# A graph layer on one Trainium2 core: edges sorted by POOL, a plan of old pairs moved by eight steps, a seed and an end on ScalarE

## The chip, the core and the metric

The kernel runs on one core of a Trainium2 chip. The core has five engines with instruction streams of their own: TensorE (PE), VectorE (DVE), ScalarE (ACT), GpSimd (POOL) and SyncE (SP), which here only issues DMAs. They meet at semaphores. SBUF is the core's working memory, PSUM holds the results of matmuls. The metric is the device time of one execution in microseconds, lower is better. Times are the median of several executions; beside them stands one execution that was recorded by the profiler, from which every duration below comes.

## What is computed

A graph with 6250 nodes and 100000 edges, 128 features each. For an edge with source `src` and destination `dst` a message is made of both nodes' features and the edge's own, normalised, passed through a relu and summed at the source node; the node's features are added and the row normalised again.

```python
x = _layernorm(x + _L0_gnn_ref(x, stack([src, dst]), edge_attr_128, W, b, gamma, beta))

def _L0_gnn_ref(x, edge_index, edge_attr, W, b, gamma, beta):
    row, col = (edge_index[0], edge_index[1])
    h = concatenate([x[row], x[col], edge_attr], axis=-1) @ W + b
    mu, var = mean(h), mean(square(h - mu))
    h = (h - mu) * rsqrt(var + 1e-5) * gamma + beta
    return segment_sum(relu(h), row, num_segments=6250)
```

The edges come sorted by destination, not by source.

## The kernel before

**Edges.** The 100000 edges are 782 tiles of 128, four to a slot, 196 slots `q` (0 to 195; the last has two tiles). In slot `q`, `edges(s, q)` (L610) makes the products of four tiles on PE, four fp32 matmuls at L619 for the edge's own features and four bf16 matmuls at L623 for the destination's; `evict` (L627) copies them to SBUF on ACT (L633); `scatters` (L639) sends each tile's 128 rows by an indirect DMA of POOL (L650) to their places in a DRAM table sorted by source. There are six tables, one for each split of the edges (`SPLITS`, L40): the last one, number 5, takes the tiles 704 to 781, slots 176 to 195.

**Ties.** Most scatters are tied to PE. At the end of slot `q`, `scatters(..., True)` issues the four tiles of slot `q - 1`, and ties them to the matmuls that PE was given since the last call (the list `done`, in which fp32 products weigh 4): the first tile to the matmul at a quarter of that work, the last to the last matmul of the slot. This holds up to slot 194; in slot 195 all that is left is issued untied. POOL's own queue is ordered by the scheduler, those of PE, DVE, ACT and SP are written out by hand. In both built programs the last four tied tiles stand in POOL's queue mixed with the six untied ones.

**Old pairs.** When a table is complete, its rows are read back by pairs of node blocks. There are 50 node blocks, so 25 pairs for a table. For the tables 0 to 4 (the old pairs) an item is one pair, or two (a twin); the last 17 items, 100 to 116, are table 4's: eight twins (100 to 107) and nine single pairs (108 to 116). `work(n)` (L1115) makes `n` steps; a step executes, for each item, those parts of its pipeline whose offset in `FLOW` (L1100) falls on this step. A new item enters every four steps. A single pair has its one-hot at offset 0 (`ones`, L748, DVE), the transposes at 2 (`turn`, L760, PE), their copy and the seed of a PSUM bank at 3 (`turned`, `seed`, L764, L770, ACT), the products with the sources' features at 5 (`pick`, L787, PE), the squares at 7 (L796, L799, ACT), the scaling at 9 (L805, L811, DVE), the sums at the nodes at 10 (`sums`, L820, PE) and their addition at 13 (`add`, L826, DVE).

**The plan.** How many steps are made in each slot follows from due points `(slot, step)` between which the plan runs straight (`due`, L1134, `steps_due`, L1139). The last two are (190, 432) and (197, 4 * 117 + ENDS); with ENDS = 0 this is (197, 468). In a slot, first come the edges' products, then one step, then the eviction, then the other steps, then the tied scatters. So what a plan changes is where the edges' products stand between the steps of the old pairs on PE, ACT and DVE. After the last slot, `work(n_tail - n_steps)` (L1245) makes the remaining steps up to number 474.

**The tail.** Table 5's 25 pairs are 14 units (`Unit`, L835) of 1, 2 x 11, 1 and 1 pairs. SP reads the rows of the first units (`load`, L843) as soon as the last scatter has landed. A unit goes through `ones`, `turn`, `turned`, `pick` (with a `seed` of the PSUM bank: an fp32 matmul with the identity on PE at L876, or a copy by ACT at L874), `square`, `root`, `scale`, `sums`, `add` as above. As its node blocks are then complete, it goes on to `begin` (times gamma), `stats`, `var`, `norm` and `end`, which scales and shifts the rows (on POOL at L972 and L973, or on DVE at L976) and issues the store of the result from SP (L978). The first unit's steps lie between the last eleven steps of the old pairs: step 474, `units[0].ones()`, step 475, `turn`, step 476, `turned`, step 477, `pick`, and so on (L1244 to L1265). At the very end the last three units b, d and c (b has two pairs, c and d one) are normalised and stored in the order b, d, c (L1295): b on POOL, d and c on DVE. The unit before them, a, is ended on POOL in both versions.

Of the kernel before, what the change touches and what calls it, by code (L numbers as in the profile page):

```python
# [12 lines left out]
AF = mybir.ActivationFunctionType  # L13
# [57 lines left out]
def col_bc(t, n):  # L71

    return t.unsqueeze(2).to_broadcast([t.shape[0], t.shape[1], n])
# [7 lines left out]
def flat(t):  # L81
    return t.rearrange("p t d -> p (t d)")


def fast_path(ctx, tc, io, bad_d, found):
# [3 lines left out]
    nc = tc.nc  # L89
# [157 lines left out]
    bias = const.tile([P, D], F32, name="bias")  # L247
# [472 lines left out]
    def load_pairs(s, p, n):  # L720

        k = 2 * SPLITS[s][1]
        rows = late["blk"].tile([P, KMAX, ROW], F32, name="hl", bufs=4)
        for i in range(n):
            nc.sync.dma_start(flat(rows[:, i * k:(i + 1) * k, :]),
                              dram_ap(sorted_d[s], (p + i) * k * P * ROW,
                                      [[k * ROW, P], [1, k * ROW]]))
        loaded[s, p] = rows
# [106 lines left out]
    class Unit:  # L835
# [130 lines left out]
            nc.vector.scalar_tensor_tensor(self.shift[:, :m], self.total[:, :m], -1.0 / D,  # L966
                                           self.frstd[:, :m], op0=ALU.mult, op1=ALU.mult)

        def end(self, last=False):
            y, m = self.y, self.m  # L970
            if not last:
                nc.gpsimd.tensor_tensor(y, y, col_bc(self.frstd[:, :m], D), op=ALU.mult)  # L972
                nc.gpsimd.tensor_tensor(y, y, col_bc(self.shift[:, :m], D), op=ALU.add)  # L973
            else:
                for j in range(m):
                    nc.vector.tensor_scalar(y[:, j, :], y[:, j, :], self.frstd[:, j:j + 1],  # L976
                                            self.shift[:, j:j + 1], op0=ALU.mult, op1=ALU.add)
            nc.sync.dma_start(io["out"][:, self.b0 * D:(self.b0 + m) * D], flat(y))  # L978
# [107 lines left out]
    n_steps = 0  # L1086
# [28 lines left out]
    def work(n):  # L1115

        nonlocal n_steps
        for _ in range(n):
            for off, step in FLOW:
                i = n_steps - LEAD - off  # L1120
                if i % 4 or not 0 <= i // 4 < len(pairs):
                    continue
                if step is None:
                    load_pairs(*pairs[i // 4])
                    continue
                if off == 0:
                    at_work[i // 4] = Pairs(i // 4, *pairs[i // 4])
                step(at_work[i // 4])
            n_steps += 1

    LEAD, ENDQ, ENDS = 6, 1, 0
    LAG = 5

    due = [(first_tile[s] // PT + LAG, 4 * first_item[s - 1]) for s in range(1, n_split)]  # L1134
# [67 lines left out]
    units = [Unit(sum(sizes[:i]), n) for i, n in enumerate(sizes)]  # L1202
# [41 lines left out]
    n_tail = 4 * (len(pairs) - 1) + LEAD + 4  # L1244
# [8 lines left out]
    work(1)  # L1253
    units[0].turned()
    work(1)
    units[0].pick(0)
    units[1].ones()
    work(2)
    units[1].turn()
    units[0].square()  # L1260
    work(5)
    assert not steps_at and not others and all(cleared[s] == NB // 2 for s in cleared)
    units[2].ones()
    units[4].load()
# [7 lines left out]
    a, b, c, d = units[-4:]  # L1272
# [21 lines left out]
    c.var()  # L1294
    for u in (b, d, c):  # L1295
        u.norm()
        u.end(u is not b)
    order.close()


@with_exitstack
def gnn_resnorm_kernel(ctx, tc, io):
    nc = tc.nc
    keep = ctx.enter_context(tc.tile_pool(name="keep", bufs=1))
    bad_t = keep.tile([1, 1], I32, name="bad_t")
    with ExitStack() as inner:
        found = []
        fast_path(inner, tc, io, bad_t, found)
    with tc.If(found[0] > 0, preferred_fallthrough_block=True, label="general"):
        with ExitStack() as inner:  # L1310
            general_path(inner, tc, io)
# [233 lines left out]
```

## Time and profile before

| what | value |
|---|---|
| median of 3 runs | 1114.98 us (1113.57 to 1116.06) |
| profiled execution | 1118.29 us |
| its span, first to last instruction | 1116.5 us |
| mean granted TensorE clock | 0.904 |
| HBM traffic | 220 GB/s over the span |
| largest group on POOL | L650, 782 scatters |
| largest groups on PE | L619 240.5 us, L820 231.3 us, L787 189.1 us |
| largest groups on ACT | L796 224.4 us, L633 113.4 us |

A row of a timeline has the start and the duration in us, the engine, line and operation, what it writes and reads, the number of instructions merged into the row, and in brackets the idle time of the engine before it and what ended it. A row of a table by windows has, for each engine, busy time and count, then the granted PE clock as a share of full speed, the DMA engines' share and GB/s. A row of grouped lines has the count, then busy us and mean ns of one, then idle time before.

### The profile page before, as it was taken

What the parts mean: (1) busy time and instruction counts of PE and PEld (TensorE: products, weight loads), DVE (VectorE), ACT (ScalarE), POOL (GpSimd) and SP (SyncE); (2) the same over time, 40 slices, a digit from 0 to 9 for tenths busy, and PEclk for the clock granted to TensorE, in tenths of its full rate; (3) what the DMA queues carried; (4) which work ended last, traced back from release to release, by engine and by line L of the source; (5) the groups of instructions that cost most, each with busy time, mean ns of one, the idle gap of its engine ahead of it and who ended that gap; (6) DMA issues with size and microseconds to landing.
All of it is one profiled execution on the core that took longest, in us unless ns stands there. A gap on an engine that the chain in (4) does not pass through costs nothing. (4 is left out here: it accounts for less than half of the span.)

```text
span 1116.5 us, 27245 instructions
## 1 busy us (share of the span) xinstructions
PE 868.9 (78%) x8880; PEld 805.1 (72%) x8880; DVE 846.0 (76%) x2364; ACT 754.6 (68%) x2983; POOL 798.5 (72%) x832
## 2 busy tenths in 40 slices
PE   6758656454887688788868688888989899987994
PEld 3657546444887678788868688887978788976773
DVE  7874656634687587768777687988898988877997
ACT  4324422115776667567767678887988999987995
POOL 2677777777777777777777777777777777774264
PEclk7788897666999899878989899998999999999998
DMA  7799999546787666667877648876877767744331
GB/s 218 230 274 267 287 312 295 185 157 205 246 282 223 218 207 204 224 205 242 277 236 239 209 147 290 268 228 223 256 245 241 232 200 248 250 144 136 124 122 61
DMA packets 128050, 247.20 MB, mean 221 GB/s; under 512 B 47005, under 2 KB 61231, under 8 KB 127897
## 3 DMA queue, kind: packets, MB, share of 16 engines
q1 hardware_dynamic: 101924, 191.92, 56.0%
q0 software_dynamic: 25104, 53.05, 13.3%
q8 instruction: 71, 1.16, 0.5%
q14 instruction: 81, 0.66, 0.2%
q10 hardware_dynamic: 870, 0.40, 0.1%
HBM read 155.49 MB, written 89.80 MB: 220 GB/s over the span
## 5 line engine op out<-in xcount | busy, mean ns | idle before, releaser
L650 POOL DMA_INDIRECT sorted<-hs,place_i x782 | 758.1, 969 | 251.0 <-issue 94.2
L787 PE MATMUL sel<-xa,ohn 128*128 128x128 bf16 x2550 | 189.1, 226 | 107.1 <-ACT sel L770 105.9
L619 PE MATMUL hp<-w,eT 128*128 128x128 f32 x1564 | 240.5, 303 | 22.0 <-ACT hs L633 22.0
L619 PEld LDWEIGHTS hp<-w,eT 128*128 128x128 f32 x1564 | 218.7, 214 | 53.0 <-issue 27.2
L787 PEld LDWEIGHTS <-ohn 128*128 128x128 bf16 x2550 | 165.4, 101 | 118.3 <-issue 99.8
L811 DVE SCALAR_TENSOR_TENSOR msg<-sel,rstd,cut 128x128 f32<-128x128 f32 x850 | 240.5, 345 | 7.9
L820 PE MATMUL pa<-msg,ohe 128*128 128x130 f32 x1700 | 231.3, 288 | 15.3 <-DVE acc L826 8.6
L796 ACT ACTIVATE sq<-sel 128x128 f32<-128x128 f32 x850 | 224.4, 282 | 27.8 <-PE sel L787 27.6
L820 PEld LDWEIGHTS pa<-msg,ohe 128*128 128x128 f32 x1700 | 210.8, 199 | 20.2 <-DVE acc L826 10.2
L796 ACT ACTIVATION_READ_ACCUMULATOR sq<-sel 128x1 f32 x850 | 180.9, 213 | 0.0
L748 DVE TENSOR_TENSOR ohe<-hl,beside 128x1024 f32<-128x1024 f32 (+2 forms) x117 | 130.2, 1113 | 21.4 <-DMA hl<-sorted 10.5
L633 ACT COPY hs<-hp 128x512 f32<-128x512 f32 x196 | 113.4, 580 | 43.5 <-PE hp L623 36.5
L770 ACT COPY sel<-hl 128x512 f32<-128x512 f32 (+1 forms) x225 | 128.1, 569 | 15.9 <-DVE msg L811 15.6
L568 ACT COPY hs<-sloc 128x12 f32<-128x12 f32 x66 | 14.1, 213 | 161.3 <-DMA sorted<-hs,place_i 158.7
L607 DVE TENSOR_SCALAR ohd<-db,part_w 128x512 bf16<-128x512 bf16 x192 | 69.1, 361 | 61.4 <-DMA db<-drel_d 47.2
L764 ACT COPY ohn<-tr 128x1024 bf16<-128x1024 bf16 (+2 forms) x117 | 107.8, 921 | 5.3 <-PE tr L760 5.3
L805 DVE RECIPROCAL rstd<-std 128x4 f32<-128x4 f32 (+1 forms) x225 | 38.2, 170 | 80.8 <-ACT std L799 79.7
L826 DVE TENSOR_TENSOR acc<-acc,pa 128x260 f32<-128x260 f32 x125 | 52.3, 418 | 54.4 <-PE pa L820 54.3
L623 PE MATMUL hp<-win,ohd 126*128 126x128 bf16 x782 | 82.0, 231 | 1.1 <-DMA win<-xb_d 1.1
L799 ACT ACTIVATE std<-ss,eps 128x4 f32<-128x4 f32 (+1 forms) x225 | 66.9, 297 | 7.3
L760 PE MATMUL tr<-ident_h,ohe 128*128 128x128 bf16 x850 | 69.4, 225 | 2.4 <-issue 2.0
L623 PEld LDWEIGHTS <-ohd 126*128 126x128 bf16 x782 | 66.2, 105 | 5.1 <-issue 1.4
(199 smaller groups left out, 1033.9 us busy)
## 6 DMA issues: line engine op xcount, KB each, us to landing
eT<-in_eT SPq DMA_DIRECT2D x96, 512.0 KB
hl<-sorted SPq DMA_DIRECT2D x75, 528.0 KB
db<-drel_d SPq DMA_DIRECT2D x96, 256.0 KB
sorted<-empty SPq DMA_DIRECT2D x100, 198.0 KB
hl<-sorted SPq DMA_DIRECT2D x50, 264.0 KB
sorted<-hs,place_i POOLq DMA_INDIRECT x782
hl<-sorted SPq DMA_DIRECT2D x25, 396.0 KB
sorted<-empty SPq DMA_DIRECT2D x50, 132.0 KB
```

Source lines behind the costliest of these rows:

```text
L619: pe(nc.tensor.matmul(hp[:, j, :], eT[:, at], w[:, 2, :], start=j == 0, stop=False, skip_group_check=True), 4)
L623: pe(nc.tensor.matmul(hp[:, j, :], oh[:3 * WN, at], win[:3 * WN, :], start=False, stop=j == m - 1, skip_group_check=True))
L633: nc.scalar.copy(hs[:, :m, 0:D], hp[:, :m, :])
L650: i = nc.gpsimd.indirect_dma_start(out=sorted_d[s][:, :], out_offset=bass.IndirectOffsetOnAxis(ap=place_i[:parts, t:t + 1], axis=0), in_=h ...
L748: nc.vector.tensor_tensor(self.ohe[:, :k, :], self.hl[:, :k, D:D + 1].to_broadcast([P, k, P]), row_bc(iota_p, k), op=ALU.is_equal)
L760: pe(nc.tensor.transpose(tr[:, j, :], half[:, j0 + j, 1::2], ident_h))
L764: nc.scalar.copy(self.ohn[:, :self.k, :], self.tr[:, :self.k, :])
L770: nc.scalar.copy(self.sel[g][:, :m, :], self.hl[:, j0:j0 + m, 0:D])
L787: pe(nc.tensor.matmul(sel[:, j, :], self.ohn[:, j0 + j, :], xa[:, b, i * D:(i + 1) * D], start=False, stop=j == m - 1 and i == 2, skip_gro ...
L796: nc.scalar.activation(sq[:, j, :], self.sel[g][:, j, :], AF.Square, accum_out=ss[:, j:j + 1])
L811: nc.vector.scalar_tensor_tensor(self.msg[:, j0 + j, 0:D], self.sel[g][:, j, :], rstd[:, j:j + 1], cut, op0=ALU.mult, op1=ALU.max)
L820: pe(nc.tensor.matmul(self.pa[:, h, :], self.ohe[:, i * k + j, :], self.msg[:, i * k + j, :], start=(j == h), stop=(j == k - 2 + h)), 4)
```

## The change

Four edits. (1) `ENDS` goes from 0 to 8: the plan's last due point is step 476 in place of 468 at slot 197, so that the old pairs' steps of the slots 190 to 195 come earlier against the edges. (2) The first unit of the tail has its PSUM bank seeded by a copy on ACT, not by a matmul on PE. (3) `end` takes an engine: b is ended on DVE in place of POOL, d on ACT in place of DVE, c on DVE as before. (4) The five steps behind the first unit are written as what is left up to step `n_tail + 11`, which is five in both versions.

```diff
-        def end(self, last=False):
+        def end(self, last=None):
             y, m = self.y, self.m
-            if not last:
+            if last is nc.scalar:
+                for j in range(m):
+                    nc.scalar.activation(y[:, j, :], y[:, j, :], AF.Identity,
+                                         bias=self.shift[:, j:j + 1],
+                                         scale=self.frstd[:, j:j + 1])
+            elif last is None:
                 nc.gpsimd.tensor_tensor(y, y, col_bc(self.frstd[:, :m], D), op=ALU.mult)
                 nc.gpsimd.tensor_tensor(y, y, col_bc(self.shift[:, :m], D), op=ALU.add)
             else:
...
-    LEAD, ENDQ, ENDS = 6, 1, 0
+    LEAD, ENDQ, ENDS = 6, 1, 8
...
-    units[0].pick(0)
+    units[0].pick(0, nc.scalar)
...
-    work(5)
+    work(n_tail + 11 - n_steps)
...
     for u in (b, d, c):
         u.norm()
-        u.end(u is not b)
+        u.end(nc.scalar if u is d else nc.vector)
```

## The prediction

> **What bounds the kernel now.** I read the page, then POOL's timeline around the last scatters, then what waited for them.
>
> ```profile
> span 1116.5 us, 27245 instructions
> L650 POOL DMA_INDIRECT sorted<-hs,place_i x782 | 758.1, 969 | 251.0 <-issue 94.2
> ```
> ```profile
> 1010.08 0.97 POOL L650 DMA_INDIRECT sorted<-hs,place_i  x1 [2.28 <-PE pa L820]
> 1011.42 0.96 POOL L650 DMA_INDIRECT sorted<-hs,place_i  x1 [0.37 <-PE sel L787]
> 1012.96 0.97 POOL L650 DMA_INDIRECT sorted<-hs,place_i  x1 [0.57 <-ACT hs L633]
> ...
> 1023.13 0.97 POOL L650 DMA_INDIRECT sorted<-hs,place_i  x1 [0.30 <-issue]
> 1024.40 0.87 POOL L650 DMA_INDIRECT sorted<-hs,place_i  x1 [0.30 <-issue]
> ```
>
> The page gives POOL 758.1 us of scatters, 0.97 us each. At the end they start 1024.40 - 1023.13 = 1.27 us apart when nothing holds them, so 782 of them fill 993 us: POOL paces most of the kernel. The row at 1024.40 is the last (tile 781, the shorter one). Counting back ten, 1011.42 is tile 771, the last of slot 192. The two rows before 1012 waited for PE: these scatters are tied to products. From 1012.96 to the end nothing waits, nine gaps of 1.27 us. So **the last scatter's start is the release of tile 771 plus ten gaps** (12.98 us, one of them 0.27 too long).
>
> What waits for the last scatter is the tail:
>
> ```profile
> 1026.54 19.64 SPq L847 DMA_DIRECT2D hl<-sorted  x15
> ```
> ```profile
> 1029.23 0.69 DVE L854 TENSOR_TENSOR ohe<-hl,beside 128x512 f32<-128x512 f32 x1 [0.95 <-DMA hl<-sorted]
> ```
>
> SP issues the first unit's load 1026.54 - 1024.40 = 2.14 us after the last scatter's start, and DVE's one-hot of it follows 2.69 us later, after an idle 0.95 us that ended with the load. DVE was there at 1028.28. So the load, and behind it POOL, already sets when the tail begins, by 0.95 us; whatever delays the last scatter delays the tail by as much.
>
> **The change, part by part.** *The plan.* The straight line from (190, 432) to (197, 468) gives 437, 442, 447, 452, 457, 462 steps after the slots 190 to 195; to (197, 476) it gives 438, 444, 450, 457, 463, 469. So the products of slot 193 come 3 steps later, of slot 194 5, of slot 195 6. The built program shows this order on PE, ACT and DVE; SP's order is the same. No instruction is added. What moves is the ties. Tile 771 is tied to the last PE product of slot 193. Before, that is the pick of step 451; after, the sums of step 456, for slot 193 now goes on to 456.
>
> ```profile
> 1003.20 1.11 PE L619 MATMUL hp<-w,eT 128*128 128x128 f32 x8
> 1004.15 0.39 PE L623 MATMUL hp<-win,ohd 126*128 126x128 bf16 x4
> 1004.37 1.11 PE L820 MATMUL pa<-msg,ohe 128*128 128x130 f32 x8
> 1005.32 0.83 PE L787 MATMUL sel<-xa,ohn 128*128 128x128 bf16 x12
> 1007.63 1.16 PE L820 MATMUL pa<-msg,ohe 128*128 128x130 f32 x8 [1.48 <-DVE acc L826]
> ...
> 1010.31 0.83 PE L787 MATMUL sel<-xa,ohn 128*128 128x128 bf16 x12
> 1010.98 1.11 PE L619 MATMUL hp<-w,eT 128*128 128x128 f32 x8
> 1011.93 0.39 PE L623 MATMUL hp<-win,ohd 126*128 126x128 bf16 x4
> 1012.15 0.39 PE L760 MATMUL tr<-ident_h,ohe 128*128 128x128 bf16 x4
> ...
> 1016.07 1.36 PE L820 MATMUL pa<-msg,ohe 128*128 128x130 f32 x8 [1.04 <-DVE msg L811]
> 1017.26 0.61 PE L619 MATMUL hp<-w,eT 128*128 128x128 f32 x4
> ...
> 1017.83 0.83 PE L787 MATMUL sel<-xa,ohn 128*128 128x128 bf16 x12
> ```
>
> The pick of step 451 is the row at 1010.31, done at 1011.14; POOL's 1011.42 follows it by 0.28. Slot 194's products are the rows at 1010.98 and 1011.93, slot 195's begin at 1017.26. The sums of step 456 are the row at 1016.07, done at 1017.43. In the changed kernel slot 194's products no longer stand in front of them: that takes away 12.15 - 10.98 = 1.17 us of PE. But slot 193's products (1003.20 to 1004.54) now come after step 449, that is just ahead of the pick at 1010.31. Where they stood they cost nothing, since PE soon after idled 1.48 us for DVE's addition; where they go, no such wait follows, and they cost their 1.17 us there. So the two nearly cancel: the sums of step 456 end at about 1017.1 (I take 0.3 us off for the copy of an eviction, ACT's smaller part). Bounds: 1016.1 if slot 193's products stay hidden, 1017.4 if nothing is saved. Then tile 771 starts at 1017.1 + 0.3 = 1017.4, and the last scatter, ten gaps of 1.27 later, at 1030.1: **5.7 us later** (4.7 to 6.0). The other ties bind less: slot 194's last one, the sums of step 460, lies some 3 us behind 1017.4, and its tile is sixth behind it in the queue, 7.6 us later. Slot 195's eviction, which feeds the last two, lies well ahead too. DVE, at the first unit's one-hot near its old 1028.3, waits until 1029.23 + 5.7 = 1034.9. Steps 475 to 485 stand behind that one-hot on DVE, so nothing useful fills the hole, and the whole tail shifts.
>
> *The clock in the hole.*
>
> ```profile
> 1028.86 0.83 PE L787 MATMUL sel<-xa,ohn 128*128 128x128 bf16 x12
> ```
>
> This is PE's last product that needs nothing of the first unit, the pick of step 475, done at 1029.69. In the changed kernel PE then has nothing until the first unit's one-hot (1034.9 + 0.69) is made, from about 1030 to 1035.6.
>
> ```profile
> 349.04 0.85 PE L787 MATMUL sel<-xa,ohn 128*128 128x128 bf16 x12 [4.47 <-ACT sel L770]
> ```
> ```profile
> 411.54 1.44 PE L787 MATMUL sel<-xa,ohn 128*128 128x128 bf16 x12 [5.11 <-ACT sel L770]
> ```
> ```profile
> 411.00:412.00 1.00, 0.46 (x5) 0.46 (x5) 0.00 (x0) 1.00 (x6) 0.74 (x1) 0.58 0.20 68
> ...
> 414.00:415.00 1.00, 1.00 (x10) 0.94 (x10) 1.00 (x3) 1.00 (x8) 0.76 (x1) 0.71 0.78 276
> ```
>
> Such holes are in the trace: after 4.47 us of idling the twelve products of a pick took 0.85 us, after 5.11 us they took 1.44, at a granted clock that fell to half within the microsecond 411 and came back within 414. With a hole of 5 to 5.6 us I take the second row: half clock for the first 3 us of the tail. In these stand only the first unit's four transposes (the size of the row at 1012.15: 0.39, so 0.27 more by the ratio of the two picks) and sums that follow DVE; the first unit's pick comes some 3 us after the transposes (the row at 1032.93 below, 3.0 behind the end of its one-hot). I put 0.2 us. Bounds: 0, and 1.3 if it lasts 5 us (the pick 1.44 - 0.85 = 0.6 more, the transposes of two units, about 1 us, by the same ratio 0.7). The Trainium skill, in "TensorE: Matmul & The Clock Gate", section Part 1, states the rule behind it: the clock halves after an idle window of about 3.4 us, and the window runs free, so its phase decides. By that rule the hole that this change opens would be paid for twice in something over half the executions; the rows above agree that near 5 us either can come.
>
> *The seed on ACT.*
>
> ```profile
> 1032.08 0.30 ACT L799 ACTIVATE std<-ss,eps 128x4 f32<-128x4 f32 x1
> 1033.80 0.28 ACT L898 ACTIVATE sq<-sel 128x128 f32<-128x128 f32 x1 [1.43 <-PE sel L887]
> ```
> ```profile
> 1032.07 1.02 PE L876 MATMUL sel<-hl,ident 128*128 128x512 f32 x2
> 1032.93 0.83 PE L887 MATMUL sel<-xa,ohn 128*128 128x128 bf16 x12
> ```
> ```profile
> L874 ACT COPY sel<-hl 128x512 f32<-128x512 f32 x2 | 1.2, 592 | 0.0
> ```
>
> PE loses 1.02 us of seed. ACT reaches its copy after the root at 1032.08, so at 1032.38, and is done 0.59 later at 1032.97: the pick starts where it did. The copy lies in ACT's idle 1.43 us. I count 0 (between -0.1 and +0.1 around it; if that cover were gone, 0.59).
>
> *The end.*
>
> ```profile
> 1106.69 0.17 DVE L966 SCALAR_TENSOR_TENSOR shift<-total,frstd 128x4 f32<-128x4 f32 x1
> ...
> 1107.23 0.56 DVE L966 SCALAR_TENSOR_TENSOR shift<-total,frstd 128x2 f32<-128x2 f32 x1
> 1107.83 1.40 DVE L976 TENSOR_SCALAR y<-y,frstd,shift 128x128 f32<-128x128 f32 x2
> 1109.15 0.15 DVE L964 RECIPROCAL frstd<-fstd 128x2 f32<-128x2 f32 x1
> 1109.41 0.16 DVE L966 SCALAR_TENSOR_TENSOR shift<-total,frstd 128x2 f32<-128x2 f32 x1
> 1109.60 0.60 DVE L976 TENSOR_SCALAR y<-y,frstd,shift 128x128 f32<-128x128 f32 x2
> ```
> ```profile
> 1107.85 1.04 POOL L973 TENSOR_TENSOR y<-y,shift 128x512 f32<-128x512 f32 x1
> ```
> ```profile
> L955 ACT ACTIVATE sq<-y,total 128x128 f32<-128x128 f32 x50 | 19.5, 390 | 3.2 <-DVE y L945 3.2
> ```
>
> Two DVE instructions take 1.40 us while POOL runs its 1.04, and 0.60 without it; a shift takes 0.56 in place of 0.16. So POOL's end of b costs DVE 0.8 + 0.4 = 1.2 us. Taken off POOL, b adds four scalings to DVE: 0.60 for two, 0.26 apart, gives 1.12 for four, from 1106.86 to about 1107.98. Then d's reciprocal and shift (1109.15 to 1109.60: 0.45) to 1108.43, then c's and its two scalings (1.05) to 1109.48, against 1110.20: **0.7 us off** (bounds 0 and 1.2). ACT ends d beside it: two instructions like L955, 0.78 us, to about 1109.2, ahead of c. The stores follow in the same order on SP.
>
> **Sum:** +5.7 + 0.2 + 0 - 0.7 = +5.2 us. The profiled execution would go from 1118.29 to 1123.5. It was 3.3 us above the median; I put the same sum on the median: 1114.98 + 5.2 = **1120.2 us**.
>
> **Rivals.** (a) *The extra steps partly fill idle time*, so tile 771's tie is later by less: five steps are 1.25 single pairs. From the pick at 1010.31 to the one that begins right behind slot 195's products, at 1017.83, two pairs and two slots' products share 7.52 us; less 1.17 and 0.57 for the products this is 2.9 a pair, so 3.6 for five steps: the tie ends at 1011.14 + 3.6 = 1014.7, the last scatter comes 3.3 us later (one gap's 0.27 is gone): 1114.98 + 3.3 - 0.7 = 1117.6. Against it: slot 193's products lose their free place.
> (b) *Not slower.* All of the moved work falls into idle time ahead of tile 771.
>
> ```profile
> 1000.00:1010.00 10.00, 7.08 (x76) 6.50 (x74) 6.72 (x22) 6.11 (x26) 5.40 (x6) 1.00 0.32 102
> ```
>
> From 1000 to 1010 ACT is busy 6.11 us and DVE 6.72 of 10, so 3.3 to 3.9 us are idle, and five steps take 3.6 us by (a). Then 771 keeps 1011.42 and only the end counts: 1114.3. It decides if the sums of step 456 end before about 1011.9. Against it: the idle time comes from additions, sums and scalings that wait for one another in a written order, which more steps do not shorten.
> (c) *The half clock lasts 5 us* and costs 1.3 in place of 0.2: 1121.3.
> (d) That the plan does nothing is ruled out by the order of the built program; edit (4) does nothing.
>
> **How the numbers follow.** Forecast 0.57 (own range 1118.5 to 1121.0: the tie's bounds, the end's, and about 1 us of scatter between runs); (c) 0.14; (a) 0.14; (b) 0.15. Differences within 0.2% (2.2 us: 1112.8 to 1117.2) are about what a measurement of this kernel cannot tell from none. Slower: forecast, (c) and 0.08 of (a), 0.79. Same: 0.06 of (a) and 0.10 of (b), 0.16. Faster: 0.05, the part of (b) for gains that I have no price for. The range takes in (a) and (c) and leaves (b) out: 1115.8 to 1122.0.
>
> **What would show it.** Right: POOL's last scatter some 5 to 6 us later against the first unit's surroundings, its wait for L820 in front of the last ten longer; DVE's wait for the first load near 6 us in place of 0.95; no L973 in the last 5 us and L976 at 0.3 us each. Wrong: a wait for the load still under 1 us with the last scatter where it was (then b), or scatters that start at less than 1.27 us, or a tail that is shorter from the first one-hot on, which would say that the seed mattered.

## The result, and the profile after

| | before | after |
|---|---|---|
| median of six runs each | 1115.26 us (1113.57 to 1117.65) | 1122.78 us (1119.40 to 1124.45) |
| ratio | | 1.0059, 95% interval 1.0044 to 1.0075 |
| profiled execution, its span | 1118.29, 1116.5 us | 1123.85, 1122.0 us |

The changed kernel is slower by 4.9 to 8.4 us (the interval times 1115). The ratio is estimated from all runs and is not the quotient of the medians, which is 1.0067; the medians are 7.52 us apart. The forecast was 5.2 us more; the profiled pair differs by 5.56 us, its spans by 5.5. The median itself, 1122.78, lies 0.8 us above the upper end of the range. Runs of one kernel are 4 to 5 us apart, and each kernel has one trace on this chip. Part of what the traces lack against the medians can be seen in them. PE of both kernels, the kernel before first, at the last products that stand in the same order in both:

```profile
996.99 0.39 PE L760 MATMUL tr<-ident_h,ohe 128*128 128x128 bf16 x4
```
```profile
994.96 0.39 PE L760 MATMUL tr<-ident_h,ohe 128*128 128x128 bf16 x4
```

PE of the changed execution is 2.03 us ahead there. It was as far ahead at 964.30 (966.34 in the kernel before), where the plans are still the same, so this head start is not the change's. Counted from these transposes, the end of the span comes 127.04 us later in the changed kernel and 119.51 before: 7.53 us more.

The page of the changed kernel: its span, and the scatters (busy, mean ns, idle before them).

```profile
span 1122.0 us, 27246 instructions
L650 POOL DMA_INDIRECT sorted<-hs,place_i x782 | 758.1, 969 | 255.8 <-issue 109.0
```

The scatters are as busy as before (758.1 us) and POOL waits 255.8 - 251.0 = 4.8 us longer ahead of them. POOL's timeline shows where: the second row is tile 771, ten places ahead of the last.

```profile
1014.26 0.96 POOL L650 DMA_INDIRECT sorted<-hs,place_i  x1 [0.45 <-PE tr L760]
1016.94 0.96 POOL L650 DMA_INDIRECT sorted<-hs,place_i  x1 [1.72 <-PE pa L820]
1018.30 0.96 POOL L650 DMA_INDIRECT sorted<-hs,place_i  x1 [0.40 <-issue]
...
1028.48 0.97 POOL L650 DMA_INDIRECT sorted<-hs,place_i  x1 [0.30 <-issue]
1029.75 0.86 POOL L650 DMA_INDIRECT sorted<-hs,place_i  x1 [0.30 <-issue]
```

Tile 771 started at 1011.42 after a pick (L787); now it starts at 1016.94 after the sums (L820). From there to the last scatter nothing waits: 1029.75 - 1016.94 = 12.81 us, ten gaps. The sums on PE that release it, and the evictions on ACT that feed the tiles behind it (slots 194 and 195):

```profile
1015.30 1.36 PE L820 MATMUL pa<-msg,ohe 128*128 128x130 f32 x8 [1.04 <-DVE msg L811]
```
```profile
1017.81 0.59 ACT L633 COPY hs<-hp 128x512 f32<-128x512 f32 x1 [0.90 <-PE hp L623]
1021.17 0.36 ACT L633 COPY hs<-hp 128x256 f32<-128x256 f32 x1
```

The sums end at 1016.66, 0.28 ahead of the scatter. Slot 194's rows are ready at 1018.40, before the second scatter behind tile 771 starts, and slot 195's at 1021.53, 7 us before the scatter at 1028.48 takes the first of them. So the tie holds POOL here, not an eviction. What waits for the last scatter, on SP's queue and on DVE:

```profile
1031.89 20.67 SPq L847 DMA_DIRECT2D hl<-sorted  x15
```
```profile
1034.78 0.69 DVE L854 TENSOR_TENSOR ohe<-hl,beside 128x512 f32<-128x512 f32 x1 [6.71 <-DMA hl<-sorted]
```

DVE is at the first unit's one-hot at 1028.07 (before: 1028.28) and now waits 6.71 us for the load, where it waited 0.95. The loss is one wait at one place.

To add it up I divide the end of both executions at four points; all are starts of rows but the fourth:

| stretch | before | after | difference |
|---|---|---|---|
| up to the first unit's one-hot (L854) | 1029.23 | 1034.78 | +5.55 |
| from there to its squares (L898) | 4.57 | 5.42 | +0.85 |
| from there to b's reciprocal (L964) | 72.68 | 72.67 | -0.01 |
| from there to the end of DVE's last instruction | 3.72 | 2.77 | -0.95 |
| from there to the end of the span | 6.30 | 6.36 | +0.06 |

The sum is +5.5 us, the difference of the spans; the first stretch has the head start of 2.03 us in it. The second stretch is the clock's. PE, then ACT, at the tail's start in the changed kernel:

```profile
1028.64 0.83 PE L787 MATMUL sel<-xa,ohn 128*128 128x128 bf16 x12
1035.53 0.61 PE L864 MATMUL tr<-ident_h,ohe 128*128 128x128 bf16 x4 [6.06 <-DVE ohe L854]
1038.66 1.44 PE L887 MATMUL sel<-xa,ohn 128*128 128x128 bf16 x12
```
```profile
1037.83 0.30 ACT L799 ACTIVATE std<-ss,eps 128x4 f32<-128x4 f32 x1
1038.03 0.58 ACT L874 COPY sel<-hl 128x512 f32<-128x512 f32 x1
1040.20 0.28 ACT L898 ACTIVATE sq<-sel 128x128 f32<-128x128 f32 x1 [1.59 <-PE sel L887]
```
```profile
1033.00:1034.00 1.00, 0.00 (x0) 0.00 (x0) 0.00 (x0) 0.00 (x0) 0.00 (x0) 0.80 0.97 264
1034.00:1035.00 1.00, 0.00 (x0) 0.00 (x0) 0.22 (x1) 0.00 (x0) 0.00 (x0) 0.50 1.00 346
...
1039.00:1040.00 1.00, 1.00 (x12) 1.00 (x10) 0.96 (x5) 0.00 (x0) 0.00 (x0) 0.50 0.41 68
1040.00:1041.00 1.00, 1.00 (x13) 1.00 (x12) 0.23 (x1) 0.80 (x7) 0.00 (x0) 0.79 0.93 330
```

The windows (each row is one microsecond, with the granted clock third from the right) put the clock at half from about 1033.6 to 1040.4. In it the transposes take 0.61 in place of 0.40 and the pick 1.44 in place of 0.83. ACT's root (L799) follows the one-hot by 3.05 us, where it was 2.85: the 0.2 of the transposes. The pick adds 0.61. Together 0.81 of the 0.85.

The end, on DVE and ACT (b's reciprocal is at 1112.87):

```profile
1113.08 0.16 DVE L966 SCALAR_TENSOR_TENSOR shift<-total,frstd 128x4 f32<-128x4 f32 x1
1113.28 1.11 DVE L981 TENSOR_SCALAR y<-y,frstd,shift 128x128 f32<-128x128 f32 x4
1114.30 0.16 DVE L964 RECIPROCAL frstd<-fstd 128x2 f32<-128x2 f32 x1
1114.50 0.16 DVE L966 SCALAR_TENSOR_TENSOR shift<-total,frstd 128x2 f32<-128x2 f32 x1
1114.58 0.17 DVE L964 RECIPROCAL frstd<-fstd 128x2 f32<-128x2 f32 x1
...
1115.04 0.60 DVE L981 TENSOR_SCALAR y<-y,frstd,shift 128x128 f32<-128x128 f32 x2
```
```profile
1114.69 0.88 ACT L973 ACTIVATE y<-y,shift,frstd 128x128 f32<-128x128 f32 x2 [0.22 <-DVE shift L966]
```

Four scalings take 1.11 us where two took 1.40 beside POOL. DVE is done at 1115.64, 2.77 after b's reciprocal, and ACT's part (to 1115.57) lies beside it.

### The profile page after: what moved, and what is told of

Read it like the earlier page. It is cut to its first block, busy times and chain, and to the rows that moved or that the text cites. A ratio compares the mean times of both kernels' runs of the same rounds, so it can differ in the third digit from the quotient of the medians.

```text
span 1122.0 us, 27246 instructions
## 1 busy us (share of the span) xinstructions
PE 872.9 (78%) x8878; PEld 809.7 (72%) x8878; DVE 846.8 (75%) x2366; ACT 754.9 (67%) x2986; POOL 796.4 (71%) x830
## 3 DMA queue, kind: packets, MB, share of 16 engines
q8 instruction: 71, 1.16, 0.4%
## 5 line engine op out<-in xcount | busy, mean ns | idle before, releaser
L650 POOL DMA_INDIRECT sorted<-hs,place_i x782 | 758.1, 969 | 255.8 <-issue 109.0
L787 PE MATMUL sel<-xa,ohn 128*128 128x128 bf16 x2550 | 190.6, 227 | 100.6 <-ACT sel L770 99.3
L787 PEld LDWEIGHTS <-ohn 128*128 128x128 bf16 x2550 | 166.9, 102 | 111.9 <-issue 95.8
L820 PE MATMUL pa<-msg,ohe 128*128 128x130 f32 x1700 | 234.1, 291 | 15.9 <-DVE acc L826 9.5
L820 PEld LDWEIGHTS pa<-msg,ohe 128*128 128x128 f32 x1700 | 213.8, 202 | 20.5 <-DVE acc L826 11.5
L799 ACT ACTIVATE std<-ss,eps 128x4 f32<-128x4 f32 (+1 forms) x225 | 66.9, 297 | 7.3
```

Source lines behind the costliest of these rows:

```text
L650: i = nc.gpsimd.indirect_dma_start(out=sorted_d[s][:, :], out_offset=bass.IndirectOffsetOnAxis(ap=place_i[:parts, t:t + 1], axis=0), in_=h ...
L787: pe(nc.tensor.matmul(sel[:, j, :], self.ohn[:, j0 + j, :], xa[:, b, i * D:(i + 1) * D], start=False, stop=j == m - 1 and i == 2, skip_gro ...
L820: pe(nc.tensor.matmul(self.pa[:, h, :], self.ohe[:, i * k + j, :], self.msg[:, i * k + j, :], start=(j == h), stop=(j == k - 2 + h)), 4)
```

## The experiments

Theory T: the loss is the tie. Five more steps stand ahead of tile 771's product, the last scatter moves by that, and DVE waits for the load. Rival E: slot 194's and 195's products and evictions were moved too, and they would hold POOL as long without the tie. Rival C: the half clock in PE's hole costs more than the 0.2 that I gave it. Rival S: the seed or the end costs, not the plan.

All experiments ran on other chips than the pair above. On these the kernel before takes 1349 to 1363 us: the engines have further idle stretches of up to 17 us there that the profile puts down to "remote", and the HBM rate is 180 GB/s in place of 220. Why is not known. Each ratio below is to the kernel before on the same chip, so it stands; but most kernels there have no wait for the first load, and this limits what they could tell. The changed kernel itself was not run there.

**The plan alone** (e1_plan; e1b_plan is the same kernel on another chip).

```diff
-    LEAD, ENDQ, ENDS = 6, 1, 0
+    LEAD, ENDQ, ENDS = 6, 1, 8
...
-    work(5)
+    work(n_tail + 11 - n_steps)
```

> Edits (1) and (4) alone: the plan's last due point at step 476, seed and ends as before. Theory (the ties move with the plan, so POOL's last scatters and behind them the first load come later): DVE waits 6 to 7 us for the first unit's load (0.95 before, 6.71 with the whole change), the clock is at half when the tail begins, the stretch from the first one-hot to b's last reciprocal is about 0.8 us longer than before's 77.25, and the end is before's 3.73 from b's reciprocal to the last DVE instruction; so the time is some 6 to 8 us above before, more than with the whole change by the 0.95 that the end gave. Rival (the loss comes from the seed on ACT or from the ends): a wait near 1 us and a time near before's.

> The plan alone (ENDS = 8) once more, to have it on the same chip as the kernels beside it. Theory: 6 to 8 us above before; DVE waits 6 to 7 us for the first load, the last scatter starts 4.8 to 5.1 us ahead of the first one-hot as in before and after, the stretch from that one-hot to b's last reciprocal is 77.9 to 78.3 us at a half clock in its first 3 to 6 us, and 3.7 us follow to the last DVE instruction. Rival: a wait near 1 us.

Measured: 1367.62 against 1363.2 us, 1.0055 (1.0027 to 1.0083); the second time 1352.15 against 1348.73, 1.0024 (1.0002 to 1.0045). POOL, then DVE, of e1_plan:

```profile
1254.04 0.97 POOL L650 DMA_INDIRECT sorted<-hs,place_i  x1 [2.32 <-PE pa L820]
...
1267.68 0.87 POOL L650 DMA_INDIRECT sorted<-hs,place_i  x1 [0.30 <-issue]
```
```profile
1274.35 1.13 DVE L811 SCALAR_TENSOR_TENSOR msg<-sel,rstd,cut 128x128 f32<-128x128 f32 x4
1275.39 0.68 DVE L854 TENSOR_TENSOR ohe<-hl,beside 128x512 f32<-128x512 f32 x1
```

The first half of T is as in the changed kernel: tile 771 (1254.04) waits for the sums L820. The second half isn't there: the one-hot's row has no bracket, it follows DVE's scaling at once, 7.71 us after the last scatter (9.72 in the second trace). DVE itself comes too late for the load to matter. So the plan alone is slower on two chips, and the wait for the load is not the reason there. From the one-hot to the first unit's squares (L898) it is 6.27 and 5.63 us in these traces, and 4.83 in e2_end and e6_untied, which have the old plan and the same seed; so 0.8 to 1.4 us may lie there. The cause stays open.

**The end alone** (e2_end), **the seed alone** (e3_seed), **both** (e4_seed_end).

```diff
-        u.end(u is not b)
+        u.end(nc.scalar if u is d else nc.vector)
```
```diff
-    units[0].pick(0)
+    units[0].pick(0, nc.scalar)
```

> Edit (3) alone: b ended on DVE, d on ACT, c on DVE; plan and seed as before. Theory: from b's reciprocal to the last DVE instruction 2.8 us in place of 3.73 (measured with the whole change: 2.78), nothing else moves, so about 0.9 us less time (0.08%), too small for the ratio but plain in the timeline. Rival: the stores of the last units set the end, and the distance from the last DVE instruction to the end of the span grows by what DVE saves (6.29 us before: 1116.5 less 1110.21).

> Edit (2) alone: the first unit's seed as a copy on ACT. Theory: the first unit's pick starts 3.7 us after its one-hot as before (1029.23 to 1032.93), so nothing is gained or lost, within 0.15 us, and the stretch from the first one-hot to b's last reciprocal stays at 77.25 within 0.3 us. Rival: that stretch gets longer by 0.6 us or more, which would put the 0.84 us that it grew with the whole change on the seed, not on the clock.

> Edits (2) and (3) without the plan (ENDS = 0). Theory: the sum of both, about 0.9 us faster than before (0.1%), DVE's wait for the first load about 1 us, the clock at full when the tail begins. Rival (seed or end carry part of the loss): slower than before by 2 us or more.

Measured, against 1363.2: e2_end 1363.59, 1.0001 (0.9976 to 1.0026); e3_seed 1362.71, a single time without an interval; e4_seed_end 1363.22, 1.0011 (0.9987 to 1.0035). Totals tell nothing at this size, but the stretches do. From b's reciprocal to DVE's end it is 2.77 or 2.78 us in all nine traces with the new end, and 3.71 to 3.73 in all five without it: the end is worth 0.95 us up to there. After that, up to the end of the span, it is 5.6 to 6.4 us with either, so no row shows the gain lost again. The seed is seen in PE's and ACT's rows, e2_end first:

```profile
1279.84 1.02 PE L876 MATMUL sel<-hl,ident 128*128 128x512 f32 x2
1280.69 0.83 PE L887 MATMUL sel<-xa,ohn 128*128 128x128 bf16 x12
```
```profile
1280.15 0.30 ACT L799 ACTIVATE std<-ss,eps 128x4 f32<-128x4 f32 x1
```

and then e3_seed:

```profile
1277.64 0.83 PE L887 MATMUL sel<-xa,ohn 128*128 128x128 bf16 x12 [0.36 <-ACT sel L874]
```
```profile
1276.81 0.30 ACT L799 ACTIVATE std<-ss,eps 128x4 f32<-128x4 f32 x1
1277.01 0.58 ACT L874 COPY sel<-hl 128x512 f32<-128x512 f32 x1
```

The root stands 3.41 us behind the one-hot in both. With the seed on PE the pick comes 1280.69 - 1280.15 = 0.54 after the root, with the copy 0.83 after it, and waits for the copy. So the seed on ACT costs 0.29 us there; e4_seed_end has the same 0.83. With the new plan it is the other way round: in both traces of the plan alone, seed on PE, the pick comes 1.25 us after the root (1279.54 to 1280.79 in e1_plan). Rival S falls as a cause of a loss of several us.

**Untied** (e5_plan_untied: the changed kernel; e5b_plan_untied the same on another chip; e6_untied: the kernel before). The scatters of the slots from 191 on are issued without a tie.

```diff
-    TIE = (12, 195)
+    TIE = (12, 191)
```

> The whole change, but the scatters from slot 191 on are issued right behind their slot's eviction and are not tied to PE products (TIE ends at 191). Theory (the ties carry the delay, not the evictions): POOL's last scatter is held only by the evictions of slots 194 and 195, so it comes 4 to 6 us earlier against DVE's arrival at the first one-hot than in the whole change; DVE's wait for the load falls from 6.7 to 1 to 3 us, the clock stays full, and the time is 4 to 6 us below the whole change. Rival (later evictions alone delay the scatters): the wait stays at 5 us or more and the time at the whole change's.

> The whole change with the scatters from slot 191 on untied, again, since on the chip of the first try the engines came later than the load in every kernel. Where the kernel before takes near 1115 us: theory (the ties carry the delay) a wait of DVE for the first load of 1 to 3 us in place of 6.7, a full clock at the tail's start, a stretch of 77.3 to 77.7 us from the first one-hot to b's reciprocal, and a time 4 to 6 us below the whole change, that is within 2 us of before. Rival (evictions): wait 5 us or more, time 5 us or more above before. Where before takes 1340 us or more: no wait in either, and nothing is told apart.

> The kernel before (ENDS = 0, seed and ends as they were) with the scatters from slot 191 on untied. Theory: POOL runs them 1.27 us apart from slot 191 on and wins the 3.2 us that it idled in front of the last ten; DVE then reaches the first one-hot before or with its load, so its wait of 0.95 us goes and about 1 us (0.1%) is gained, no more, since DVE's own work ahead sets the start. Rival (the ties spare PE or the DMA engines something): the work ahead of the tail gets longer and the time rises by 2 us or more.

Measured: e5_plan_untied 1355.92 against 1348.73, 1.0045 (1.0013 to 1.0077); e5b_plan_untied 1367.85 against 1363.03, 1.0033 (1.0008 to 1.0059); e6_untied 1354.24 against 1348.73, 1.0032 (1.0003 to 1.0061). POOL's waits in e6_untied:

```profile
1227.17 0.96 POOL L650 DMA_INDIRECT sorted<-hs,place_i  x1 [3.54 <-ACT hs L633]
...
1244.98 0.96 POOL L650 DMA_INDIRECT sorted<-hs,place_i  x1 [7.59 <-ACT hs L633]
...
1251.40 0.97 POOL L650 DMA_INDIRECT sorted<-hs,place_i  x1 [1.64 <-ACT hs L633]
```

Without the tie POOL waits for evictions instead (5.8, 6.6 and 2.8 us in e5b_plan_untied). DVE still has no wait for the load, so nothing could be won at the tail, and both kernels are slower than the kernel before. The two untied runs of the new plan have no tied run with the same seed and end beside them. On these chips rival E describes what stands behind the tie. On the first chip untying wasn't tried, but its trace speaks against E. In e5_plan_untied and e5b_plan_untied the last scatter starts 6.62 and 6.64 us behind the end of slot 194's eviction; in the changed kernel that eviction ends at 1018.40, so with the evictions alone the last scatter would start near 1025.0. That is an estimate; it is 4.7 us ahead of 1029.75, and 0.6 behind the 1024.40 of the kernel before.

**A warm clock** (e7_warm; e7b_warm the same on another chip): twenty matmuls without use ahead of the first unit's transposes, in the changed kernel.

```diff
+    warm_up(20)
     units[0].turn()
```

> The whole change with twenty matmuls of 512 columns that nothing reads in front of the first unit's transposes, to keep PE busy in the hole. Theory (of the 0.84 us by which the tail is longer from the first one-hot to b's reciprocal, the half clock is the cause): the granted clock stays at 1.00 through the first unit, its pick takes 0.83 us in place of 1.44, and the stretch is 77.2 to 77.5 us again; DVE's wait for the load stays near 6.7 us. Rival (the seed on ACT or the loads are the cause): the stretch stays at 78.0 us or more with a full clock.

> The whole change with twenty idle matmuls ahead of the first unit's transposes, again. Where the kernel before takes near 1115 us and PE has its hole of 6 us: theory (half clock) a granted clock of 1.00 through the first unit, its pick in 0.83 us, the stretch from the first one-hot to b's reciprocal 77.5 us in place of 78.09, DVE's wait still near 6.7 us, the time up to 0.6 us below the whole change. Rival: 78.0 us or more at full clock, and the seed or the loads carry it. Where before takes 1340 us or more, there is no hole and the matmuls cost about 4 us, as on the first try.

Measured: 1359.83 against 1348.73, 1.0087 (1.0052 to 1.0122), and 1369.85 against 1363.03, 1.0062 (1.0036 to 1.0088). PE in e7_warm, whose one-hot starts at 1260.57 without a wait:

```profile
1261.86 0.83 PE L787 MATMUL sel<-xa,ohn 128*128 128x128 bf16 x12
1262.53 4.50 PE L1009 MATMUL hp<-ones_h 128*128 128x512 bf16 x20
1266.87 0.39 PE L864 MATMUL tr<-ident_h,ohe 128*128 128x128 bf16 x4
```

There was no hole to fill, so the matmuls stood in PE's way: 82.80 us from the one-hot to b's reciprocal, against 77.9 to 78.6 with the same plan, seed and end. Inconclusive on rival C.

**Sixteen steps further** (e10_plan16), **and untied** (e11_plan16_untied), from the changed kernel. This moves the tie and the evictions further still, and puts two more steps ahead of the first one-hot (476 steps are made by the end of slot 195).

```diff
-    LEAD, ENDQ, ENDS = 6, 1, 8
+    LEAD, ENDQ, ENDS = 6, 1, 16
```

> The whole change with the suspected cause doubled: ENDS = 16 in place of 8, so that slot 193's last PE product, to which tile 771 is tied, is the sums of step 460, one more pair late, and step 475 and 476 stand ahead of the first one-hot. Theory (ties): POOL's row of tile 771 is released by L820 and the last scatter follows 12.7 to 13 us later; DVE waits for the first load also on the chips where it did not wait with ENDS = 8: 8 us where before takes near 1115 us, 2 to 6 us where it takes 1350; the first one-hot comes 4.8 to 5.1 us after the last scatter. The time is 2 to 4 us above the whole change. Rival (engines, not the load, start the tail on such a chip): no wait, first one-hot 7 us or more after the last scatter.

> As the run beside it (ENDS = 16), with the scatters from slot 191 on untied. Theory (ties): only the evictions hold POOL, the last two scatters follow slot 195's, and the last one comes about 4 us earlier against DVE's arrival at the first one-hot than in the tied run; the wait is 0 to 2 us and the time 2 to 5 us below the tied run. Rival (the later products and evictions themselves are the delay): the same wait and the same time as in the tied run, within 1 us.

Measured against 1349.6: 1352.15, 1.0011 (0.9990 to 1.0033), and with `TIE = (12, 191)` as well 1354.37, 1.0050 (1.0026 to 1.0074). The profiled spans go the other way, 1349.7 and 1347.7. That untying gains 2 to 5 us is not borne out. But the wait for the load is back. DVE and then PE of e10_plan16, whose last scatter starts at 1258.07:

```profile
1262.83 0.69 DVE L854 TENSOR_TENSOR ohe<-hl,beside 128x512 f32<-128x512 f32 x1 [2.10 <-DMA hl<-sorted]
```
```profile
1263.57 0.61 PE L864 MATMUL tr<-ident_h,ohe 128*128 128x128 bf16 x4 [2.11 <-DVE ohe L854]
1265.35 1.44 PE L887 MATMUL sel<-xa,ohn 128*128 128x128 bf16 x12 [1.17 <-ACT sel L874]
```

and POOL's, then DVE's rows of e11_plan16_untied:

```profile
1255.41 0.96 POOL L650 DMA_INDIRECT sorted<-hs,place_i  x1 [2.50 <-ACT hs L633]
1256.67 0.87 POOL L650 DMA_INDIRECT sorted<-hs,place_i  x1 [0.30 <-issue]
```
```profile
1261.59 0.69 DVE L854 TENSOR_TENSOR ohe<-hl,beside 128x512 f32<-128x512 f32 x1 [2.71 <-DMA hl<-sorted]
```

In the four traces with a wait, the one-hot follows the last scatter by 4.83 us (before), 5.03 (after), 4.76 and 4.92 (these two). In the ten without one DVE comes 6.7 to 9.7 us behind the last scatter. That is the condition of T, seen from both sides on several chips: the last scatter sets the tail when DVE is less than about 4.9 us behind it. DVE came 3.88 behind it before, and 1.68 ahead of it after. In e11_plan16_untied the last two scatters are held by slot 195's eviction: there, E holds. In e10_plan16 the tie is not alone either: its tile 771 starts at 1243.63 behind sums, but the last scatter follows after 14.44 us, where 12.7 to 13 were expected, with waits of 1.65 (put down to slot 195's products) and 0.69 us between. The half clock after the hole is in both traces, transposes 0.61 and pick 1.44 as in the changed kernel: C's mechanism repeats. From the squares to b's reciprocal it is 72.66 to 72.71 us in ten traces (before, after, and e1 to e6 with their repeats), and 74.08 and 73.64 in these two: there the granted clock is still 0.50 in the microsecond after the squares have begun, which may be the reason.

No kernel here is shown to beat the kernel before. Taking the two edits without the plan (e4_seed_end) is within the noise.

## Why the prediction was right, and where its sizes were off

**The bound.** Right: the tail began with the last scatter's load, DVE already waited 0.95 us for it, and what delayed the scatter delayed the end. That is shown by the first pair of traces, and its condition by the 4.9 us above. It is not a property of the kernel alone: on the other chips it doesn't hold at this plan.

**The plan.** Right in mechanism; that the size came out so near is in part luck. Tile 771 at 1016.94 (forecast 1017.4), released by the sums of step 456, which ended at 1016.66 (forecast 1017.1); ten gaps; the last scatter +5.35 (5.7), the one-hot +5.55. But counted from the transposes at 996.99 and 994.96, that is without the head start, the last scatter comes 7.38 us later. And on the way to the tie lies a cost that the sum put at nothing, a half clock from 1006.3 to 1009.7 (see the last section): from the sums at 1005.86 to the products behind the next sums, at 1009.86, it is 4.00 us on PE, where it was 2.68 (1007.63 to 1010.31). These 1.3 us and the forecast 5.7 make 7.0 of the 7.4. The clock left out and the head start nearly cancel.

That the tie and not the evictions set this is read from the trace of the changed kernel, where the rows lie ready; the experiment that was to show it, untying, met chips where the load wait is absent or the evictions bind. The share of the plan in the median is therefore argued from traces, not isolated by a run. Rival (a), less delay, and rival (b), none, fall by the same rows.

**The clock in the hole.** The step of the tail that was mis-sized most: 0.2 in place of 0.8 us. I took half clock for 3 us of the tail and left the first unit's pick out of it. It lasted from 1033.6 to 1040.4, and the pick at 1038.66 fell into it. Rival (c) had this length, at 1.3: it counted two units' transposes, and only the first unit's lay on the path. One of the two rows by which I weighed the hole was misread. Behind the hole of 4.47 us at 349.04 the clock did fall, only later than the pick. PE of the kernel before:

```profile
349.71 3.66 PE L820 MATMUL pa<-msg,ohe 128*128 128x130 f32 x16
```

Sixteen such products take 2.00 us elsewhere (339.16), and the granted clock is 0.86 in the microsecond from 349 and 0.50 from 350 to 353. In the kernel before, every hole on PE of 3.1 us or more has half clock in it or within 2.1 us behind it. So the question was not whether the clock falls, but when it falls and comes back. The Trainium skill, "TensorE: Matmul & The Clock Gate", Part 1, says that the clock comes back after a busy window of about 3.4 us. Here 1040.4 - 1035.5 = 4.9 us went by, of work with gaps at first; in the last 3.4 of them, from 1037.0, PE was busy 3.3 us, so the trace agrees.

**The seed.** 0 forecast, 0 here: the pick follows the root's start by 0.83 us (before 0.85). But the cover was thin. Two chains meet at the pick, PE's sums and seed, and ACT's root and copy; before, they ended together. In e2_end against e3_seed ACT's is 0.29 us longer. At half clock it is PE's: the sums ended at 1038.52, and the two fp32 products of a seed put off the next product by 1.46 us at half clock in e10_plan16 (1269.27 to 1270.73). By an estimate from these rows the pick would have begun near 1039.8 with the seed on PE, 1.1 us later than it did. No run isolates this.

**The end.** 0.95 in place of 0.7 us. The four scalings came out as worked out (1.11 for 1.12); the two reciprocals and shifts of d and c took 0.74 us (1114.30 to 1115.04) where I had added 0.90, since d's and c's overlap.

**The sum.** +5.55 + 0.85 - 0.95 + 0.05 against +5.7 + 0.2 - 0.7: the errors nearly cancel, and so do those inside the 5.55. The range missed the median by 0.8 us because it was drawn about one profiled pair's sum with some 1 us for the runs, while the medians moved by 7.5.

## What to carry to other kernels

Before background work is put ahead of the last producers, ask what those producers are tied to: here five cheap steps moved the product that releases a queue of ten 1.27 us scatters, and a wait of 0.95 us became one of 6.7. A change of 1 us among runs that differ by 5 is judged by dividing the trace at points that each edit moves, not by totals, and from the last rows that the edits leave alone. And a hole opened on PE is paid a second time in the products right behind it, so price the first of these at half clock when they are on the path.

## What the hardware did that was not expected

The clock was halved after short holes too. PE of the changed kernel, some 30 us before the tail, and the windows about it:

```profile
1005.86 1.73 PE L820 MATMUL pa<-msg,ohe 128*128 128x130 f32 x8 [2.15 <-DVE acc L826]
1008.11 1.92 PE L820 MATMUL pa<-msg,ohe 128*128 128x130 f32 x8
```
```profile
1006.00:1007.00 1.00, 1.00 (x7) 1.00 (x8) 0.00 (x0) 0.00 (x0) 0.00 (x0) 0.64 0.00 0
1007.00:1008.00 1.00, 1.00 (x7) 0.69 (x6) 0.37 (x2) 0.00 (x0) 0.56 (x1) 0.50 0.00 0
```

After 2.15 us of idling, and with PE already at work again, the clock fell within the microsecond 1006; the sums took 1.73 and 1.92 us in place of 1.16. The plan made this hole longer: 1.48 us stood here before (ahead of 1007.63), when slot 193's products still lay in front of it. In e10_plan16 a hole of 2.11 us was enough as well; in the kernel before, five holes of 2.0 to 2.8 us went without a loss.

When the clock changes can be worked out from the shares in such windows. In the changed kernel it fell at 1006.28, came back at 1009.70, fell at 1033.60 and came back at 1040.42. These points are 3.42, 23.90 and 6.82 us apart, 1, 7 and 2 times 3.41; in the kernel before, 411.16 and 414.58 are 3.42 apart. Up to the tail's end every stretch of half clock in the two traces lasts 1, 2, 3 or 4 times 3.41 us. So in these traces the clock changes only at points of a grid. Between two such points, from 1002.87 to 1006.28, PE was busy 1.26 us, and the clock fell at the end; from 1033.60 to 1037.01 it was busy 1.19 us, and the clock stayed at half; from 1037.01 to 1040.42 it was busy 3.27 us, and the clock came back. What a hole costs here thus depends also on where it lies on the grid.

The same kernel takes 1115 us on one chip and 1349 to 1363 on others, with engines held for up to 17 us at a time. The traces name no cause.
